# A graph layer on one core: moving the transposes of the attention weights to just in front of each part's sum, two parts ahead, and spreading the logits over four parts

## The chip, the core and the metric

The kernel runs on one core of one Trainium2 chip. The metric is the device time of one execution in microseconds (us). The kernel before takes 1484.36 us, the median of three runs (1482.55 to 1485.34).

The engines named below work side by side, each through its own list of instructions in order: TensorE (PE, matrix products and transposes into PSUM), ScalarE (ACT), VectorE (DVE), GpSimd (POOL), and SyncE, which starts transfers.

## The reference, cut to what matters

```python
def _top_p_attention(X, W1, W2, W3):
    q = X @ W1.T @ W2.T
    k = X @ W3.T
    probs = softmax(q @ k.T, axis=-1)
    # keep, row by row, the largest probabilities until their sum reaches TOP_P = 0.9
    A = probs * mask
    return A / A.sum(-1, keepdims=True)

h = relu(layernorm(x))                    # (3327, 256)
R = (adj + eye) / row sums                # adj is sparse: about 5 entries in a row
Xf = Xa = h; Z = 0
for n in range(2):                        # STEPS = 2
    A = _top_p_attention(Xa, W1, W2, W3)
    Xf = R @ Xf
    Xa = A @ Xa
    Z = Z + Xf @ U1[n].T + Xa @ U2[n].T
return x + layernorm(h + Z) * ln_g + ln_b
```

`A` has 3327 x 3327 entries. The kernel pads the rows to 26 tiles of 128 (`NT = 26`, `NP = 3328`) and never holds `A` as a whole: it goes tile by tile, and for one tile of 128 rows it holds `e`, the 128 x 3328 exponentials of the logits.

## The kernel before: the parts that the change touches

Each of the two steps is one loop over the tiles. One pass of it (an *iteration* `i`) is cut into seven *parts*, `PARTS = 7`. In every part a few pieces of work for different tiles are taken up in the order that a string of letters (`PLAN`) gives; each letter advances one generator to its next `yield`. In iteration `i` of the first step the tile `i` has its threshold found and its weights masked (`d`), the tile `i+1` is measured (`m`), the logits of tile `i+2` are made (`w`), the queries of tile `i+3` are projected (`q`), the tile `i-2` is spread through the sparse matrix (`s`) and finished (`e`), and the sum `A @ Xa` of the tile before is made, four of its 26 column blocks in each part.

```python
AHEAD = (1, 2)
PLAN = (("mdsssa", "mdsssa", "edawwp", "sda", "mpdea", "mdgawwq", "emdgq"),   # first step
        ("cmss", "cnms", "wwnfd", "mdsss", "smwqdfg", "mqdfg", "mwdf"))       # second step
LATE = (1, 4)
    ...
            for k in range(PARTS):
                g = PARTS * (i - 1) + k - LATE[step]
                summing = valid(g // PARTS)
                if summing:
                    sums.turn(g, min(i, NT - 1))
                for c in "bb" + (LAST.get(i, PLAN[1]) if step else PLAN[0])[k]:
                    next(work[c], None)
                if summing:
                    ended = sums.sum(g)
    ...
            for c in "cnwqsepgb" if step else "dmwqsepgb":
                run(work[c])          # what is left of the iteration's work
```

The two functions that make the sum. `turn` transposes 128 x 128 blocks of `e` into a PSUM tile `pt` and lets ACT copy them to `eT` in SBUF; `sum` multiplies with `eT`. The PSUM tile `pt` has two buffers, used in turn by every user of `ps_t`; `eT` has three.

```python
ps_t = ctx.enter_context(tc.tile_pool(name="ps_t", bufs=2, space=PSUM))
ps_l = ctx.enter_context(tc.tile_pool(name="ps_l", bufs=2, space=PSUM))
    ...
def turn(self, g, made):
    while self.turned <= min(g + self.ahead, PARTS * (made + 1) - 1):
        ...
        pt = ps_t.tile([P, 4, P], F32, tag="pt", name="pt")
        for j in range(w):
            PE.transpose(pt[:, j, :], e[:, (j0 + j) * P : (j0 + j + 1) * P], ident)
        eT = tpool.tile([P, 4, P], F32, tag="eT", name="eT", bufs=3)
        S.copy(eT[:, :w, :], pt[:, :w, :])
def sum(self, g):
    ...
    for c in range(4 * k, min(4 * k + 4, NT)):
        PE.matmul(self.pa, eT[:, c - 4 * k, :], self.xa[:, j, :], start=c == 0, stop=c == NT - 1)
    if k < PARTS - 1:
        return None
    S.activation(dst[:n], self.pa[:n], AF.Copy, scale=...)       # xa, the tile's sum
```

The other users of a `pt` buffer, and the work that stands between them, shortened (V is DVE, S is ACT, G is POOL; a `# yield` is where a letter ends):

```python
# w and q: one generator, weights(t): q takes its first two pieces, w the four that follow
PE.matmul(pq[:, 0, :], w2d[qp, :], qry[qp, j, :]); PE.matmul(pm, qry[qp, j, :], qm[...])   # pt
S.copy(qT, pq[:, 0, :]); S.copy(mq, pm)                               # yield
V.scalar_tensor_tensor(mq ...); six small G operations -> ms          # yield
for n in range(4):                                                    # the logits, 832 columns each
    pl = ps_l.tile(...); two PE.matmul(pl[:, a, :416], qT, keys)
    S.activation(e[...], pl, AF.Exp, accum_out=za)                    # yield after each piece
# e: first_end(i - 2)
aT = transposed(r)                  # 2 PE.transpose into pt, S.copy(xT)   yield
PE.matmul(pz, aT, u2) x2            # 512 columns, PSUM tile of its own
S.copy(xw[:, t, :], pz[:, D:]); V.tensor_tensor(sv, pz[:, :D], x0) # yield
PE.matmul(pk ...) x2 (and 2 more in even tiles)    # pt
S.copy(krs) (even tiles); S.copy(keys); S.copy(qry)                   # yield (even tiles)
PE.matmul(pg ...); S.copy(gt)                      # pt, even tiles only
# m: measured_once(tile i + 1)
nine small S operations             # yield
S.activation(ja, e, AF.Relu)        # a pass over 128 x 3328             yield
S.activation(ja, e, AF.Sign)        # a second such pass                 yield
seven small S operations            # yield
five small V operations
# d: settle(tile i), all on V: a pass w over e; ten MAX8; ten MAX8; three rounds; two rounds;
#    the mask e = e * (e >= threshold), a pass over e; two small operations (a yield between each)
# p: packed(i + 1):   PE.matmul(pb) in pt, S.copy                     yield   V operations
# g: gathered(i):     PE.matmul(po) in pt, S.copy(lo)                 yield   V operations, then
#                     ten indirect DMAs on G that fetch the rows of the sparse matrix and of bx
# s: spread(i - 2):   six PE.matmul(pr), a yield after each; then V operations
# a: listed():        one chunk of adj by DMA, V.tensor_reduce        yield
```

All instructions of PE, ACT and DVE keep the order of this text.

Of the kernel before, what the change touches and what calls it, by code (L numbers as in the profile page):

```python
# [22 lines left out]
NT = (N + P - 1) // P  # L23
# [299 lines left out]
SQG, SQK = ((c[0], c[1] / (2 * c[0]), c[2] - c[1] ** 2 / (4 * c[0])) for c in (PG, PK))  # L323
HALF = NT // 2
PARTS = -(-NT // 4)
AHEAD = (1, 2)
COUNTED = [t for t in range(NT - 2) if t % 2 == 0]
EARLY = (11, 18, NT)
FIRST = 8 * P
# [14 lines left out]
def guess_graph_layer(ctx, tc, x, adj, w1t, w2t, w3t, u1t, u2t, ln_g, ln_b, out, flag):  # L344
# [207 lines left out]
    def weights(step, t, live, known=True):  # L552

        r = dict(Z=rec[:, step, 3, t : t + 1])
        qT, r["ms"] = yield from project(step, t, law=known)
        yield
        r["e"] = e = es[(2, 3, 0, 1, 4, 5)[t % 6] if step else t % 4]
        r["za"] = za = small.tile([P, CUT + 1], F32, tag="za", name="za")
        live[step, t] = r
        w = HALF * P  # L560
        wd = w // CUT
        for n in range(CUT):
            c = n * wd
            pl = ps_l.tile([P, 2, 512], F32, tag="pl", name="pl")
            for a in range(2):
                p = slice(a * DA, (a + 1) * DA)
                PE.matmul(pl[:, a, :wd], qT[p, :],  # L567
                          keys[step][p].rearrange("p a b -> p (a b)")[:, c : c + wd],
                          start=True, stop=True)
            if n < CUT - 1:  # L570
                S.activation(e.rearrange("p (a n) -> p a n", a=2)[:, :, c : c + wd], pl[:, :, :wd],  # L571
                             AF.Exp, accum_out=za[:, n : n + 1])
                yield
            else:
                S.activation(e.rearrange("p (a n) -> p a n", a=2)[:, :, c : w - 1], pl[:, :, : wd - 1],
                             AF.Exp, accum_out=za[:, n : n + 1])
                S.activation(e[:, w - 1 : w], pl[:, 0, wd - 1 : wd], AF.Exp, accum_out=za[:, n + 1 :])
# [110 lines left out]
    def measured(step, r):  # L688
        return measured_twice(r) if step else measured_once(r)
# [52 lines left out]
    def prove(step):  # L742
        v8, t, tn, Z = (rec[:, step, k, :] for k in range(4))
        ok = small.tile([P, NT], F32, tag="cum", name="ok", bufs=1)
        o2 = small.tile([P, NT], F32, tag="dr", name="o2", bufs=1)
        V.tensor_tensor(ok, v8, t, ALU.is_lt)
        V.tensor_tensor(o2, tn, t, ALU.is_lt)
        V.tensor_tensor(ok, ok, o2, ALU.mult)
        for a, c, op in ((tn, 0.0, ALU.is_gt), (t, 0.5 * BIG, ALU.is_lt),
                         (Z, 1.0e-30, ALU.is_gt), (Z, BIG, ALU.is_lt)):  # L750
            V.scalar_tensor_tensor(ok, a, c, ok, op, ALU.mult)
        V.tensor_scalar(ok, ok, 0.5, None, ALU.is_lt)
        n = N - (NT - 1) * P
        f = small.tile([P, 1], F32, tag="f", name="f")
        V.tensor_reduce(f, ok[:, : NT - 1], AX.X, ALU.add)
        V.tensor_tensor(fl, fl, f, ALU.add)
        V.tensor_tensor(fl[:n], fl[:n], ok[:n, NT - 1 :], ALU.add)
        if step == 0:
            V.tensor_scalar(ok, lists[:, :, LIST - 1], 0.0, None, ALU.is_gt)
            V.scalar_tensor_tensor(ok, ends, float(P), ok, ALU.is_gt, ALU.add)  # L760
            V.tensor_reduce(f, ok, AX.X, ALU.add)
            V.tensor_tensor(fl, fl, f, ALU.add)
# [121 lines left out]
    def first_end(t):  # L884
        aT = transposed(live.pop(("r", t)))
        yield
        pz = ps_r.tile([P, 2 * D], F32, tag="pr", name="pz")
        for c in range(ND):
            PE.matmul(pz, aT[:, c, :], u2[:, c].rearrange("p n d -> p (n d)"), start=c == 0, stop=c == ND - 1)  # L889
        S.copy(xw[:, t, :], pz[:, D:])  # L890
        sv = row.tile([P, D], F32, tag="sv", name="sv", bufs=2)
        V.tensor_tensor(sv, pz[:, :D], x0[:, t, :], ALU.add)  # L892
        nc.sync.dma_start(sx[t], sv)
        yield
        yield from prep(1, aT, t)
# [32 lines left out]
    def run(work, n=99):  # L928
        for _ in range(n):
            next(work, None)  # L930
# [59 lines left out]
    def spread(step, t):  # L990
        rr = rrs[:, t : t + 1]
        own = row.tile([P, D + 1], F32, tag="own", name="own", bufs=2)
        nc.sync.dma_start(*((own[:, :D], vx[:, t, :]) if step else (own, bx[:, t, :])))
        s1 = row.tile([P, D], F32, tag="s1", name="s1", bufs=4)
        nc.sync.dma_start(s1, (sx if step else ax)[t])
        a, w = acs.pop(t), D + 1 - step
        pr = yield from diffuse(a, xgs.pop(t), own[:, :w], w)
        if step == 0:
            nc.sync.dma_start(cx[t], a.rearrange("p k r -> p (k r)"))
        yield  # L1000
        if step == 0:
            V.reciprocal(rr, pr[:, D : D + 1])
        V.scalar_tensor_tensor(s1, pr[:, :D], rr, s1, ALU.mult, ALU.add)  # L1003
        if step == 0:
            nc.sync.dma_start(vx[:, t, :], s1)
        else:
            live["f", t] = s1

    def refetch(t):
# [7 lines left out]

    PLAN = (("mdsssa", "mdsssa", "edawwp", "sda", "mpdea", "mdgawwq", "emdgq"),  # L1020
            ("cmss", "cnms", "wwnfd", "mdsss", "smwqdfg", "mqdfg", "mwdf"))

    LAST = {NT - 1: ("cfss", "cn", "ndddddd", "sss", "sf", "f", "f"), NT: ("cf", "v", "", "", "f", "f", "fv")}
# [4 lines left out]
    for step in range(2):  # L1028
        sums = Sums(step, live, xw if step else x0, AHEAD[step])

        for i in range(-1, NT + 2):
            if step == 0 and i == NT - 3:
                begun = [weights(1, t, live, False) for t in range(3)]
            if step == 1 and i == -1:
                run(begun[0])
                prove(0)
                for e in es[4:]:
                    G.memset(e[:, N:NP], 0.0)
            work.update(
                n=work["m"],  # L1040
                c=work["d"],
                d=settle(step, i, live[step, i]) if valid(i) else none,
                m=measured(step, live[step, i + 1]) if valid(i + 1) else none,
                s=spread(step, i - 2 + 2 * step) if valid(i - 2 + 2 * step) else none,
                w=later.pop((step, i + 2), none),
                e=first_end(i - 2) if step == 0 and valid(i - 2) else none,
                a=lister if step == 0 and i else none,
                p=packed(i + 1) if step == 0 and i >= 0 and valid(i + 1) else none,
                g=none if not valid(i + 2 * step) else refetch(i + 2) if step else gathered(i),
                b=none, q=none, v=proof() if step and i == NT else none,  # L1050
            )
            if i >= 0 and valid(i + 3):
                later[step, i + 3] = weights(step, i + 3, live)
                work["q"] = itertools.islice(later[step, i + 3], 2)
            if step == 0 and i >= NT - 2 and i < NT + 1:

                work["w"] = itertools.islice(begun[i - NT + 2], CUT - 1)
            if step == 0 and i >= NT - 3 and i < NT:
                work["q"] = itertools.islice(begun[i - NT + 3], 1)
            if i == -1:  # L1060
                work["w"] = itertools.chain(begun[1], begun[2])
            if step == 0 and i < 1:
                work["b"] = itertools.islice(product, EARLY[i + 2] - EARLY[i + 1])
            if step == 1 and i == -1:
                work["g"] = itertools.chain(refetch(0), refetch(1))
            for k in range(PARTS):
                g = PARTS * (i - 1) + k - LATE[step]
                summing = valid(g // PARTS)
                if summing:
                    sums.turn(g, min(i, NT - 1))  # L1070
                for c in "bb" + (LAST.get(i, PLAN[1]) if step else PLAN[0])[k]:
                    next(work[c], None)
                if summing:
                    ended = sums.sum(g)
                    if ended and step == 0:
                        live["r", ended[0]] = ended[1]
                    elif ended:
                        work["f"] = finish(ended[0], live.pop(("f", ended[0])), ended[1])
            for c in "cnwqsepgb" if step else "dmwqsepgb":
                run(work[c])  # L1080
            if step == 0 and i == NT:
                moments(1)
                for t in range(3):
                    live[1, t]["ms"] = returned(project(1, t, queries=False))
# [50 lines left out]
```

## Time and profile before

The profile was taken of one execution of 1556.6 us. A profiled execution is longer than a timed one here, so shares and waits are read from the profile, and the time from the three runs.

| stretch of the profile, us | what runs | PE busy | DVE busy | ACT busy | POOL busy |
|---|---|---|---|---|---|
| 0 to 150 | layer norm, first keys and products | 103.76 | 82.08 | 79.00 | 55.77 |
| 250 to 400 | first step, its middle | 132.00 | 121.79 | 102.18 | 82.21 |
| 800 to 900 | end of the first step | 92.39 | 50.53 | 47.91 | 41.73 |
| 1050 to 1200 | second step, its middle | 136.84 | 134.67 | 132.75 | 130.00 |

The first sum of the first step begins at 152.3 us and its last at 893.7 us (the matmuls `pa<-x,eT`); those of the second step (`pa<-xw,eT`) run from 953.0 us to 1543.5 us. In the middle of the first step an iteration takes 29.0 us: the matmul `pk`, which comes once in an iteration, starts at 466.24 us and, twelve iterations later, at 813.76 us.

A busy share is an average. What the first step waits for is read from the list of waits of each engine and from the timeline of one iteration; the lines of both are shown with the prediction. In a line of the timeline the columns are: start, duration, engine, line of the kernel, operation, output and inputs, count, and in brackets how long the engine had been idle before it and who ended that idle time. A row of several matmuls is merged; since they are pipelined, what a group costs PE is read from the start of one row to the start of the next.

### The profile page before, as it was taken

Reading aid. Unit: us, or ns where it says so; the run is one execution under the profiler, and the core shown is the slowest. Engines: PE = TensorE matmul, PEld = TensorE weight load, DVE = VectorE, ACT = ScalarE, POOL = GpSimd, SP = SyncE. Lnnn points to the kernel's source line nnn. Section 1 sums busy time; section 2 is a strip of 40 time slices with the busy share of each in tenths; the row PEclk is TensorE's granted clock in tenths of the full one; section 3 lists DMA queues with packets and bytes.
Section 4 is the critical chain, followed back from the end, with each engine's and each line's share of the span. In section 5 each row is a group of like instructions: output and inputs, shape, how many; then the busy total and the mean of one; then the engine's idle time right before and its main releaser. Section 6 shows DMA issues by size and latency. Waiting matters only on the chain.

```text
span 1556.6 us, 22648 instructions
## 1 busy us (share of the span) xinstructions
PE 1320.4 (85%) x6495; PEld 988.6 (64%) x6495; DVE 1230.2 (79%) x3837; ACT 1104.6 (71%) x2476; POOL 990.8 (64%) x1489
## 2 busy tenths in 40 slices
PE   5857888888888989979889937989989989998886
PEld 3523666666666667657667725767767667777675
DVE  4457797977988889779787238989888889898894
ACT  5537576676676676767665378988988988988961
POOL 6312555645756646556555156888888888888851
PEclk9978899999999999999999967999999999999998
DMA  7554343533533534434323131221221221222200
GB/s 220 167 163 134 105 139 96 152 105 96 156 109 107 143 105 116 127 106 130 114 65 89 53 88 31 72 79 55 72 75 49 81 67 57 82 65 59 82 18 20
DMA packets 97687, 149.81 MB, mean 96 GB/s; under 512 B 15985, under 2 KB 60528, under 8 KB 97552
## 3 DMA queue, kind: packets, MB, share of 16 engines
q1 hardware_dynamic: 78400, 104.00, 21.7%
q0 software_dynamic: 16640, 42.69, 10.6%
q10 hardware_dynamic: 2512, 1.57, 0.3%
q8 instruction: 54, 0.88, 0.2%
q14 instruction: 81, 0.66, 0.2%
HBM read 120.93 MB, written 27.28 MB: 95 GB/s over the span
## 4 chain that ended last, share of the span: by engine, by line
PE 34%; POOL 23%; ACT 20%; DVE 9%; issue 7%; DMA 4%; another core or an unknown queue 1%; SPq 0%; POOLq 0%; ACTq 0%; DVEq 0%
PE pa L793 15%; ACT ja L600 8%; POOL xg L868 7%; PE pt L779 4%; POOL g L678 4%; PE pr L876 4%; PE pl L567 4%; DMA at<-in_adj 3%; ACT e L571 3%; PE pz L889 2%; ACT eT L781 2%; DVE e L734 1%; PE pk L487 1%; DVE cand L705 1%; POOL rstd L468 1%
## 5 line engine op out<-in xcount | busy, mean ns | idle before, releaser
L781 ACT COPY eT<-pt 128x512 f32<-128x512 f32 (+1 forms) x364 | 201.8, 555 | 226.2 <-PE pt L779 145.9
L793 PE MATMUL pa<-xw,eT 128*128 128x256 f32 x1352 | 331.8, 387 | 29.2 <-ACT xa L800 28.6
L793 PE MATMUL pa<-x,eT 128*128 128x256 f32 x1352 | 348.2, 401 | 5.6 <-ACT eT L781 4.5
L859 POOL DMA_INDIRECT ac<-in_adj,index x130 | 176.7, 1359 | 249.2 <-DVE mq L541 152.3
L600 ACT ACTIVATE ja<-e,g 128x3328 uint8<-128x3328 f32 x106 | 325.8, 3073 | 0.1
L793 PEld LDWEIGHTS pa<-xw,eT 128*128 128x128 f32 x1352 | 250.0, 191 | 91.9 <-ACT xa L800 33.3
L793 PEld LDWEIGHTS pa<-x,eT 128*128 128x128 f32 x1352 | 258.7, 199 | 59.9 <-issue 14.5
L705 DVE MAX8 cand<-w 128x8 f32<-128x168 f32 (+1 forms) x1040 | 251.2, 317 | 0.0
L779 PE MATMUL pt<-ident,e 128*128 128x128 f32 x1144 | 179.9, 278 | 39.5 <-DVE e L734 22.9
L868 POOL DMA_INDIRECT xg<-bx,index x130 | 165.9, 1276 | 47.6 <-issue 33.4
L779 PEld LDWEIGHTS pt<-ident,e 128*128 128x128 f32 x1144 | 143.6, 144 | 79.0 <-issue 32.5
L567 PE MATMUL pl<-k,qT 64*128 64x416 f32 x832 | 186.2, 552 | 4.5 <-ACT qT L531 4.0
L700 DVE SCALAR_TENSOR_TENSOR w<-e,g 128x3328 f32<-128x3328 f32 x44 | 163.9, 3725 | 0.7
L876 PE MATMUL pr<-xg,ac 128*128 128x257 f32 (+1 forms) x520 | 138.6, 390 | 22.8 <-DVE s L1003 20.2
L868 POOL DMA_INDIRECT xg<-vx,index x130 | 128.2, 986 | 44.0 <-issue 35.1
L811 DVE TENSOR_REDUCE fm<-at 128x4 f32<-128x512 f32 (+1 forms) x182 | 115.8, 637 | 49.2 <-DMA at<-in_adj 47.3
L734 DVE SCALAR_TENSOR_TENSOR e<-e,rec 128x3328 f32<-128x3328 f32 x40 | 147.4, 3684 | 0.0
L571 ACT ACTIVATE e<-pl 128x832 f32<-128x832 f32 x132 | 113.4, 867 | 7.5 <-PE pl L567 6.9
L876 PEld LDWEIGHTS pr<-xg,ac 128*128 128x128 f32 x520 | 91.0, 195 | 33.6 <-DVE s L1003 20.5
L567 PEld LDWEIGHTS pl<-k,qT 64*128 64x128 f32 x832 | 71.0, 189 | 51.0 <-issue 41.2
L712 DVE MAX8 bb<-cand 128x8 f32<-128x160 f32 x286 | 92.7, 324 | 6.4
L892 DVE TENSOR_TENSOR sv<-pz,x 128x256 f32<-128x256 f32 x26 | 11.0, 422 | 91.4 <-ACT xw L890 81.2
(226 smaller groups left out, 2213.5 us busy)
## 6 DMA issues: line engine op xcount, KB each, us to landing
at<-in_adj SPq DMA_DIRECT2D x156, 256.0 KB
cx<-ac SPq DMA_DIRECT2D x26, 384.0 KB
ac<-cx SPq DMA_DIRECT2D x26, 384.0 KB
bx<-e SPq DMA_DIRECT2D x26, 128.5 KB
own<-bx SPq DMA_DIRECT2D x26, 128.5 KB
x<-in_x SPq DMA_DIRECT2D x13, 256.0 KB
xr<-in_x SPq DMA_DIRECT2D x26, 128.0 KB
ax<-e SPq DMA_DIRECT2D x26, 128.0 KB
```

What stands on the lines that cost most here:

```text
L567: PE.matmul(pl[:, a, :wd], qT[p, :], keys[step][p].rearrange("p a b -> p (a b)")[:, c : c + wd], start=True, stop=True)
L571: S.activation(e.rearrange("p (a n) -> p a n", a=2)[:, :, c : c + wd], pl[:, :, :wd], AF.Exp, accum_out=za[:, n : n + 1])
L600: S.activation(ja, e, f, bias=guess, scale=sign, accum_out=total)
L700: V.scalar_tensor_tensor(w, e, col(16), e, ALU.is_lt, ALU.mult, accum_out=d2)
L705: V.max(cand[:, 8 * s : 8 * s + 8], w[:, s * SEG : min(NP, (s + 1) * SEG)])
L734: V.scalar_tensor_tensor(e, e, at(1), e, ALU.is_ge, ALU.mult, accum_out=ra)
L779: PE.transpose(pt[:, j, :], e[:, (j0 + j) * P : (j0 + j + 1) * P], ident)
L781: S.copy(eT[:, :w, :], pt[:, :w, :])
L793: PE.matmul(self.pa, eT[:, c - 4 * k, :], self.xa[:, j, :], start=c == 0, stop=c == NT - 1)
L859: G.indirect_dma_start(out=ac[:, k, :], out_offset=None, in_=rows, in_offset=bass.IndirectOffsetOnAxis(ap=index[:, t, k : k + 1], axis=0), ...
L868: G.indirect_dma_start(out=xg[:, k, :w], out_offset=None, in_=rows, in_offset=bass.IndirectOffsetOnAxis(ap=index[:, t, k : k + 1], axis=0))
L876: PE.matmul(pr[:, :w], ac[:, k, :], own if k == KT - 1 else xg[:, k, :w], start=k == 0, stop=k == KT - 1)
```

## The change: what it does and what it is for

Three things change, all in the first step. The transposes are made two parts ahead of the sum, not one. They stand directly in front of the part's sum, behind the other work of the part, and not at the head of the part; so ACT can copy them while PE multiplies. And the four pieces of the logits are made in four different parts (2, 3, 5 and 6) and not in two pairs (parts 2 and 5), so that ACT doesn't get two exponentials at once. With that the plan is arranged anew: the keys of the finished tile (`pk`) move from part 6 to part 5, their product `pg` from the end of the iteration to part 6, and the projection of the queries (`pq`) from part 5 to part 6.

```diff
-AHEAD = (1, 2)
+AHEAD = (2, 2)
@@
-    PLAN = (("mdsssa", "mdsssa", "edawwp", "sda", "mpdea", "mdgawwq", "emdgq"),
+    PLAN = (("mdsssa", "mdsssa", "ewpda", "wsda", "mpdea", "mwedga", "wmdegq"),
             ("cmss", "cnms", "wwnfd", "mdsss", "smwqdfg", "mqdfg", "mwdf"))
@@
             for k in range(PARTS):
                 g = PARTS * (i - 1) + k - LATE[step]
                 summing = valid(g // PARTS)
-                if summing:
+                if summing and step:
                     sums.turn(g, min(i, NT - 1))
                 for c in "bb" + (LAST.get(i, PLAN[1]) if step else PLAN[0])[k]:
                     next(work[c], None)
+                if summing and not step:
+                    sums.turn(g, min(i, NT - 1))
                 if summing:
                     ended = sums.sum(g)
```

## The prediction, made before the changed kernel was run

> **What bounds the kernel now.** I read the busy times by stretch first, then the list of waits of PE, then the timeline of one iteration on PE, ACT and DVE. In the middle of the first step PE is the busiest engine:
>
> ```profile
> 400.00:550.00 150.00, 129.42 (x654) 98.06 (x653) 123.00 (x393) 101.39 (x247) 92.47 (x116) 0.98 0.42 121
> ```
>
> The columns are length, PE, weight loads, DVE, ACT, POOL, clock, DMA share and GB/s. No engine is full: PE is idle for some 20 of 150 us, DVE for 27. So the order of the work and its waits set the pace. The list of PE's waits over 175 to 840 us, which is nearly the whole first step, says which:
>
> ```profile
> PE pq L526 <- ACT eT L781: 37.3, 21, 2.9
> PE pk L487 <- ACT mq L535: 24.2, 15, 2.4
> PE po L844 <- ACT eT L781: 8.2, 6, 1.5
> ...
> PE pk L487 <- ACT qT L531: 3.3, 2, 1.7
> ```
>
> The numbers are us in all, times, longest. None of the four is a wait for data. `pq`, `pk` and `po` each want one of the two `pt` buffers and wait until ACT has copied its last content out. They make 37.3 + 24.2 + 8.2 + 3.3 = 73.0 us in 665 us. An iteration takes (813.76 - 466.24) / 12 = 29.0 us, so these are 23 iterations with 3.2 us each. The first step has 26: some 83 us of the profiled 1556.6 are all that better placing can take from these waits.
>
> The timeline shows how they come about. First PE, then ACT:
>
> ```profile
> 454.70 0.60 PE L779 MATMUL pt<-ident,e 128*128 128x128 f32 x4
> 455.14 1.88 PE L889 MATMUL pz<-u,xT 128*128 128x512 f32 x4
> 456.86 1.89 PE L793 MATMUL pa<-x,eT 128*128 128x256 f32 x8
> 458.59 0.60 PE L779 MATMUL pt<-ident,e 128*128 128x128 f32 x4
> 459.02 0.29 PE L844 MATMUL po<-lists,oh 128*128 128x13 f32 x2
> 459.25 1.67 PE L567 MATMUL pl<-k,qT 64*128 64x416 f32 x8
> 461.65 0.48 PE L526 MATMUL pq<-qry,w2d 64*128 64x128 f32 x2 [0.74 <-ACT eT L781]
> ...
> 462.29 1.99 PE L793 MATMUL pa<-x,eT 128*128 128x256 f32 x8
> 464.12 0.38 PE L779 MATMUL pt<-ident,e 128*128 128x128 f32 x2
> 466.24 0.71 PE L487 MATMUL pk<-xT,wk 128*128 128x128 f32 x4 [1.74 <-ACT mq L535]
> ```
>
> ```profile
> 455.88 3.07 ACT L600 ACTIVATE ja<-e,g 128x3328 uint8<-128x3328 f32 x1
> 458.94 0.36 ACT L890 COPY xw<-pz 128x256 f32<-128x256 f32 x1
> 461.01 0.59 ACT L781 COPY eT<-pt 128x512 f32<-128x512 f32 x1 [1.71 <-PE pl L567]
> 461.50 0.30 ACT L621 ACTIVATE g<-oa,g 128x1 f32<-128x1 f32 x1
> ...
> 465.88 0.31 ACT L535 COPY mq<-pq 128x130 f32<-128x130 f32 x1
> ```
>
> The reader is to see that parts 4 and 5 are heavy for ACT: a pass of 3.07 us, a copy, seven small operations, two exponentials, two copies; PE runs into them through the two buffers. And one thing that the work doesn't explain: the transposes issued by 459.02 were copied only at 461.01, though ACT had ended `xw` by 459.30. In the next iteration it is larger: transposes issued at 481.18, ACT free from 480.38, the copy at 486.30. I call this the late copy: about 2 to 4.5 us, once in an iteration, always near parts 3 to 5. The profile shows no cause. The ten gathers that POOL issues run just then (477.67 to 486.47 us in that iteration), but that is only a coincidence in time so far.
>
> DVE sets a floor. Its pass `w<-e,g` starts at 440.77 and at 466.41 us, 25.64 us apart, with 0.63 us idle in between: 25.0 us of DVE work in an iteration. PE's own work, summed from the spacing of its rows, is: transposes 6 x 0.44 + 0.22 = 2.9, sum 6 x 1.73 + 0.86 = 11.2, sparse matmuls 6 x 0.43 = 2.6, logits 4 x 0.83 = 3.3, `pz` 1.7, and `pq`, `pk`, `pg`, `po`, `pb` and the transposes of `xT` about 2.2 together: 23.9 us.
>
> **What the Trainium skill says.** "TensorE: Matmul & The Clock Gate", Part 2, step-by-step: matmuls stay in program order, only weight loads are pulled ahead. So PE can't go round a matmul that waits for a buffer; the trace agrees, behind the `pq` of 461.65 stood a sum whose `eT` had been there since 455.99. "PSUM — Partial Sum Buffer", Specifications: eight banks of 2 KiB per partition. A `pt` is 4 x 128 x 4 bytes, one bank; with two of two banks for `pl` and one each for the two sums all eight are taken, which is why a third `pt` isn't the simple way out. No run here shows that limit. "Perfetto Trace Analysis", Tensor Engine Instruction: the end of a matmul is estimated, and the semaphore update comes only when PSUM has acknowledged the write. That leaves room for a late copy behind a matmul that looks done; the trace has delays of 0.26 us normally (issued 455.14, copied 455.40) and of 2.0 and 4.7 us in the two cases above.
>
> **The change, part by part.** It removes no work and adds none: 23.9 us on PE, 25.0 on DVE and about 20 on ACT remain. It moves three things.
>
> First, transposes ahead of the sum. In ACT's list nothing changes by this alone: a copy that stood at the head of part k+1 stands now at the end of part k, behind the same work. On PE the transposes pass in front of one sum, so the copy can start 1.73 us earlier, and between a copy's transposes and the next user of a buffer there is always a sum. With nothing else changed this should take nearly all of the waits.
>
> Second, single logits. One exponential (0.85 us) goes from part 2 to 3 and one from 5 to 6; part 3 had ACT idle for 1 to 5 us. Neutral to good.
>
> Third, the new places of `pk` and `pq`, which I work out. Take the end of issue of part 3's transposes as 0. PE: sum 1.73, `pz` 1.72, transposes 0.44 (3.89), sum 1.73, `pl` 0.83 (6.45), `pk` 0.55 (7.00), `po` 0.23 (7.23); the next transposes want the buffer of `pk`. ACT: copy from 0.26 to 0.74, Sign pass 3.06 to 3.80, `xw` 0.26 to 4.06, copy of the part-4 transposes from 4.15 to 4.63, seven small operations 2.36 (461.50 to 463.86) to 6.99, exponential 0.85 to 7.84, keys and queries 2 x 0.27 to 8.38. With 0.15 us from ACT to PE the transposes start at 8.53: **a new wait of 1.3 us**. For the kernel before, the same reckoning from the part-4 transposes: PE is at `pk` after 3.89 + 0.23 + 1.66 + 0.64 + 1.83 + 0.38 = 8.63; ACT ends `mq` at 4.63 + 2.36 + 0.05 + 1.68 + 0.30 = 9.02, so `pk` at 9.17: 0.5 us of wait without a late copy. The other 2.7 of the 3.2 us come from the late copy. So the new plan gives back 0.8 us of what the earlier transposes win.
>
> Now with a late copy of 4.4 us on part 4's transposes. Before: `po` waits until 5.29 (1.4), `pq` until 9.1 (1.9), `pk` until 13.5 (1.5): 4.8. After: its copy ends at 9.03, `po` waits from 7.00 to 9.18 (2.2), keys are copied at 12.8, the transposes wait from 9.41 to 12.95 (3.5): 5.7. If the late copy falls on part 1 instead, the two-part lead takes it: sum 1.73, `xT` 0.3 and `pl` 0.83 stand in front of the next use, and a delay of up to some 2 us costs nothing. Where it will fall I can't tell.
>
> Sum for an iteration: at best 3.2 us of waits fall to the 1.3 of the new wait and 0.2 besides, minus 1.7 us or 44 us over 26 iterations; at worst the late copy stays in part 4, plus 0.9 us or 23 us. I take minus 0.3 us, 8 us in all: **1476 us**.
>
> **Rivals.** (a) The late copy vanishes or is hidden wholly, and the step runs at DVE's floor with a little on top, 26 us in place of 29: 78 us less, some 1406. For it: the two-part lead is meant for just that, and part of the 72 us by which the profiled execution is longer may sit in these waits, so that less is there to gain. Against it: the buffers are still two. (b) The wait moves to the transposes behind `pk`, as worked out, and eats the gain: 1476 to 1508. For it: ACT does the seven small operations and the exponential first, in order. (c) DVE becomes the bound. `q`'s second piece, which needs `mq`, follows its first at once now, with the large pass behind it; the wait for `mq` could be 1 us or more of DVE, which has 4 us free. It makes (a) smaller, not (b) larger.
>
> **Range and chances.** The best case without (a) is 1440, the worst 1508; with some of (a) the low end is 1438. Faster by over 2% needs 1.1 us less in each iteration, which asks that the late copy be mostly hidden: 0.22. Slower by over 2% needs 1.1 us more, past my worst case: 0.1. The rest, 0.68.
>
> **What would show it.** In the waits of PE, `pq` and `pk` should be nearly gone and transposes `pt L779` waiting for ACT's `qry` or `k` copy (line 497 or 496) should stand in their place, 1 to 3.5 us each iteration. ACT's busy time and DVE's in the step should stay; DVE should wait for `mq`. The distance of two `pk` should be 28 to 30 us; 26 would speak for (a). The second step should not move. I am wrong if the transposes don't wait for the keys' copies, or if the late copy goes away with the new order.

## The result, and the profile after

The changed kernel takes **1496.26 us** (median of four runs, 1495.4 to 1496.74). In the same set of runs the kernel before takes 1484.85 us. The ratio is 1.0078 with a 95% interval of 1.006 to 1.0095: a loss of 11.4 us, where a gain of 8 us was forecast.

The runs were made on several chips, on three of the five used for the experiments the kernel before takes about 1570 us and not 1485, and so times are compared only with the kernel before on the same chip, by a ratio that leaves out executions more than 1.5% above the fastest of their kernel.

The busy times by stretch of the changed kernel, with the same columns as in the prediction:

```profile
400.00:550.00 150.00, 142.98 (x733) 105.61 (x732) 139.07 (x451) 114.38 (x280) 89.96 (x126) 1.00 0.48 132
```

Beside the line of before this looks like a gain: PE 142.98 us busy in place of 129.42, DVE 139.07 in place of 123.00. It should have made me suspicious of the line of *before*: that profile is of an execution of 1556.6 us. The waits of PE over 175 to 840 us, again us in all, times, longest:

```profile
PE pt L779 <- ACT qry L497: 23.4, 24, 1.2
...
PE pt L779 <- ACT gt L504: 4.3, 11, 0.4
```

`pq`, `pk` and `po` wait for no buffer any more. In their place the part-5 transposes wait for the buffer of `pk` until ACT has copied the queries out. The timeline of PE and then of ACT at that place:

```profile
437.46 0.97 PE L567 MATMUL pl<-k,qT 64*128 64x416 f32 x4
438.36 0.71 PE L487 MATMUL pk<-xT,wk 128*128 128x128 f32 x4
438.91 0.29 PE L844 MATMUL po<-lists,oh 128*128 128x13 f32 x2
440.41 0.44 PE L779 MATMUL pt<-ident,e 128*128 128x128 f32 x2 [1.21 <-ACT qry L497]
```

```profile
438.68 0.29 ACT L627 ACTIVATE g<-g 128x1 f32<-128x1 f32 x1
438.88 0.84 ACT L571 ACTIVATE e<-pl 128x832 f32<-128x832 f32 x1
...
440.09 0.26 ACT L497 COPY qry<-pk 64x128 f32<-64x128 f32 x1
```

ACT does the last of the seven small operations, the exponential of the part's single piece of logits and then the copies, in order. The wait is 1.21 us in one iteration and 0.74 in the next (even tiles have a longer `pk`).

The mean distance of two sums' ends (the copies `xa<-pa`) in the first step is 25.80 us. In the second step it is 22.68, and 22.7 in the kernel before: the step that the change doesn't touch didn't move. So the question is what the first step of the kernel before really looks like when it takes 1484 us.

### The profile page after: what moved, and what is told of

Same layout as the page of the kernel before. It is cut to its first block, busy times and chain, and to the rows that moved or that the text cites. A ratio compares the mean times of both kernels' runs of the same rounds, so it can differ in the third digit from the quotient of the medians.

```text
span 1493.7 us, 22652 instructions
## 1 busy us (share of the span) xinstructions
PE 1307.2 (88%) x6495; PEld 969.0 (65%) x6495; DVE 1227.8 (82%) x3837; ACT 1108.2 (74%) x2476; POOL 987.6 (66%) x1489
## 3 DMA queue, kind: packets, MB, share of 16 engines
q0 software_dynamic: 16640, 42.69, 11.4%
## 4 chain that ended last, share of the span: by engine, by line
PE 33%; POOL 24%; ACT 24%; DVE 7%; issue 7%; DMA 4%; SPq 0%; ACTq 0%; POOLq 0%; DVEq 0%
PE pa L793 15%; ACT ja L600 10%; POOL xg L868 8%; PE pl L567 5%; PE pr L876 5%; POOL g L678 5%; PE pt L779 5%; ACT e L571 4%; DMA at<-in_adj 3%; ACT eT L781 3%; POOL rstd L468 1%; PE pz L949 1%; POOL xr L906 1%; DVE cand L705 1%; DVE fm L811 1%
## 5 line engine op out<-in xcount | busy, mean ns | idle before, releaser
L793 PE MATMUL pa<-x,eT 128*128 128x256 f32 x1352 | 325.3, 383 | 0.0
L793 PEld LDWEIGHTS pa<-x,eT 128*128 128x128 f32 x1352 | 245.4, 192 | 26.1
L859 POOL DMA_INDIRECT ac<-in_adj,index x130 | 133.1, 1024 | 188.0 <-DVE index L852 139.3
L779 PE MATMUL pt<-ident,e 128*128 128x128 f32 x1144 | 183.5, 281 | 69.9 <-ACT qry L497 23.4
L779 PEld LDWEIGHTS pt<-ident,e 128*128 128x128 f32 x1144 | 138.4, 144 | 129.6 <-issue 57.7
L868 POOL DMA_INDIRECT xg<-bx,index x130 | 181.3, 1394 | 49.7 <-issue 33.3
L567 PE MATMUL pl<-k,qT 64*128 64x416 f32 x832 | 199.7, 565 | 4.3 <-ACT qT L531 3.8
L876 PEld LDWEIGHTS pr<-xg,ac 128*128 128x128 f32 x520 | 94.8, 194 | 36.8 <-DVE s L1003 21.0
L567 PEld LDWEIGHTS pl<-k,qT 64*128 64x128 f32 x832 | 66.8, 188 | 59.7 <-issue 50.6
L575 ACT ACTIVATE e<-pl 128x830 f32<-128x830 f32 x44 | 37.6, 854 | 73.4 <-PE pl L567 73.3
```

The lines of the kernel that those rows point to most:

```text
L567: PE.matmul(pl[:, a, :wd], qT[p, :], keys[step][p].rearrange("p a b -> p (a b)")[:, c : c + wd], start=True, stop=True)
L859: G.indirect_dma_start(out=ac[:, k, :], out_offset=None, in_=rows, in_offset=bass.IndirectOffsetOnAxis(ap=index[:, t, k : k + 1], axis=0), ...
L868: G.indirect_dma_start(out=xg[:, k, :w], out_offset=None, in_=rows, in_offset=bass.IndirectOffsetOnAxis(ap=index[:, t, k : k + 1], axis=0))
L876: PE.matmul(pr[:, :w], ac[:, k, :], own if k == KT - 1 else xg[:, k, :w], start=k == 0, stop=k == KT - 1)
```

## The experiments

### The kernel before once more: which kernel did the first profile show?

The theory at this point: the late copies of the prediction are a property of the execution and not of the kernel, and the first profile was of another kind of execution than the three timed runs. Rival: the late copies are in the kernel before always, the new order took them away, and the loss has another source, large enough to eat 80 us. There is no edit: it is the kernel before, unchanged, on three chips.

> The kernel before, unchanged, for a second profile. Theory A (the late copies belong to that one profiled execution and not to the kernel): the profiled span is near 1483 us, no copy eT starts more than 1 us after its transposes and ACT are both free, and an iteration of the first step takes 25.2 to 25.6 us, not 29. Rival (the late copies belong to the kernel, and the change removed them): the span is near 1556 us again and an iteration takes 28 to 29 us. Timed: ratio 1.000 to the kernel before under both.

> The kernel before, unchanged, for a profile beside runs in which it takes 1485 us. Expected there: no late copy of eT; PE's waits for pq and po gone; only pk waits for the copy mq, about 0.5 us an iteration (the reckoning without late copies); 25.3 us an iteration (25.8 of the changed kernel less 11.4 us over 26). If the waits for pq and po are still there without late copies, my reading of the first profile was right and only their size was off. If the kernel before is at 1570 us, late copies are expected again.

> The kernel before, for its profile. Where it takes 1485 us: no late copies, no waits of PE for pq and po, 0.5 us of wait for pk in an iteration, 25.3 us an iteration. Where it takes 1570: late copies as in the two profiles so far.

Measured: 1571.27 us on the first chip (ratio to the kernel before 0.9995, interval 0.9969 to 1.0021), 1571.11 us on the second (1.001, 0.9987 to 1.0033), 1483.23 us on the third (0.9981, 0.9971 to 0.9992). The last ratio is of a kernel with itself: differences of 0.2% are not read as effects here. The first two profiles came out as the rival has it (spans of 1566.9 and 1568.9 us, with late copies), but there the timed runs take 1570 us as well; the third, of an execution of 1483.1 us, settles it.

I counted in each trace the copies `eT` of the first step that start more than 0.6 us after their transposes have ended and ACT is free. There are 31 in the profile that the prediction read (some 92 us of delay in all), 28 to 30 in each of the other two above 1550 us (some 91 to 93 us), and none in the execution of 1483 us. (The end of a transpose in the trace is modelled, so such a count can be off by two or three.) In every kernel that has any they fall on the fourth to sixth of a tile's seven groups of transposes, which the kernel before makes in parts 3 to 5.

The granted clock differs as well: over 200 to 800 us it was 0.97, 0.95 and 0.95 in the three profiles with late copies and 1.00 in the one without. At 3 to 5% of 600 us that is 18 to 30 us of PE's time at most, by estimate, so the clock alone doesn't make the difference of 85 us. Nor do late copies need the lower clock: `pk` apart, below, has about 10 of them at 1.00. Which of the two brings the other was not separated.

The waits of PE in the execution of 1483 us (200 to 800 us), then those of DVE:

```profile
PE pk L487 <- ACT mq L535: 21.2, 21, 1.1
PE pz L889 <- DVE s L1003: 5.3, 5, 1.7
PE pk L487 <- ACT qT L531: 1.6, 2, 1.1
```

```profile
DVE fm L811 <- DMA at<-in_adj: 11.0, 13, 1.8
```

The waits of `pq` (37.3 us in the first profile) and `po` (8.2) do not exist there. Only the wait in front of `pk` is left, about 1.0 us an iteration. And the chain of work that ended last, cut out of the same profile (start, us, engine, tile, line, count):

```profile
438.14 3.61 DVE e L734 x2
441.78 0.16 DVE ra L735
441.94 0.58 DVE fm L811
...
444.28 3.62 DVE w L700 x2
447.92 0.21 DVE need L701
448.13 0.59 DVE fm L811
448.73 2.28 DVE cand L705 x10
451.00 3.05 DMA at<-in_adj
454.08 0.43 DVE fm L811
...
463.32 3.61 DVE e L734 x2
```

**DVE is the bound.** From one mask pass to the next the chain is DVE and a transfer that DVE waits for: 463.32 - 438.14 = 25.2 us, beside 25.0 us of DVE's own work (in these 25.2 us DVE is busy for 24.15; the rest of its work is short gaps between its instructions). PE's wait of 1.0 us at `pk` lies beside this chain and costs nothing: the kernel `place_only` below hasn't got it, and its iteration is as long. In the first profile the same chain ran mostly over PE (58% of its length between 250 and 700 us, ACT 24%, DVE 9%); in this one DVE has 77% and PE nothing. So the first step of the kernel before, as it was timed, had next to nothing to give to a better order of PE's work.

### The changed kernel once more

> The changed kernel, unchanged, timed again beside the kernel before on one chip. In the last session the kernel before took 1570 us and its profile held 28 late copies of eT (91.6 us in all) in parts 3 to 5 of the first step; the profile of the changed kernel held none. Theory A (late copies come with the chip or the session, and the changed kernel is slower by its buffer wait wherever there are none): if the kernel before is near 1485 here, the changed one is near 1496; if it is near 1570, the changed one has late copies too and lies at 1560 to 1600. Theory B (the new order is free of late copies everywhere): near 1496 in both cases.

> The changed kernel. Where the kernel before takes 1485 us: 1496 again, ratio 1.008. Where it takes 1570: it holds late copies too, and since q_late took 1532 there, 1530 to 1540; then the changed kernel is slower on the one and faster on the other.

Measured: 1496.57 us (1.0091, 1.0074 to 1.0108) and 1496.86 us (1.0067, 1.0044 to 1.0091), without late copies. The second is the median of four, one of which took 1924.12 us; that of the other three is 1496.34 us. The loss is there on both chips where the kernel before takes 1485 us; the changed kernel wasn't run on a chip where that one takes 1570, so what the two expectations say of that stays untested. The chain of the changed kernel, one iteration, from the wait behind `pk` to the next:

```profile
440.09 0.27 ACT qry L497
440.41 0.44 PE pt L779 x2
440.84 1.73 PE pa L793 x8
442.57 0.90 PE pl L567 x4
...
452.52 0.90 PE pl L567 x4
...
455.96 0.92 PE pl L567 x4
456.91 0.59 ACT e L571
...
457.86 0.47 ACT eT L781
458.33 3.04 ACT ja L600 x2
...
465.60 0.27 ACT qry L497
465.91 0.44 PE pt L779 x2
```

The bound has gone over to a **loop of PE and ACT**: the copy of the queries lets PE go on (440.41), PE works through 16.5 us of rows in order up to the logits of part 3 (455.96), ACT takes the exponential of that piece, the copy of the transposes, the Sign pass, the seven small operations, the exponential of part 5 and the copies of keys and queries (456.91 to 465.87, 9.0 us), and PE goes on again. PE has 61 to 62% of the chain between 250 and 700 us, ACT 35%, DVE none. The loop takes 25.5 or 26.4 us by turns, DVE needs 25.0.

### The logits in single pieces alone

The kernel before with nothing but its four logits pieces in four parts (each `w` in a part of its own):

```diff
-    PLAN = (("mdsssa", "mdsssa", "edawwp", "sda", "mpdea", "mdgawwq", "emdgq"),
+    PLAN = (("mdsssa", "mdsssa", "edawp", "swda", "mpdea", "mdgawq", "emwdgq"),
```

> The kernel before with the logits in four single pieces (parts 2, 3, 5 and 6) and nothing else moved. Theory: ACT's two exponentials in part 5 stand in the way of mq, which pk waits for, and so one of them moved to part 6, ahead of nothing that is waited for, should cut the wait of pk from about 0.5 us to 0; but the buffer of pb in part 2 comes one logit piece sooner to PE, and waits for a copy behind the Relu pass, 0.5 to 0.8 us. The reckoning gives plus 0.5 us an iteration, 1490 to 1500 us where the kernel before takes 1485. Rival (single logits are what helps): 1470 to 1480.

Measured: 1500.17 us, 1.0112 (1.0095 to 1.0129): a loss of 15.9 us without any of the rest. The time is at the upper end of the expected range, and the wait of `pb` came; that of `pk` fell from 1.0 to 0.7 us and not to 0:

```profile
PE pk L487 <- ACT mq L535: 14.9, 21, 0.7
PE pb L832 <- ACT eT L781: 10.1, 22, 0.5
```

Its chain, by engine and line:

```profile
by line: ACT ja L600 24.2%; PE pa L793 22.0%; ACT eT L781 8.2%; PE pl L567 7.0%; PE pt L779 5.6%; issue 5.4%; ACT e L571 3.2%; PE pk L487 2.7%; ACT g L622 1.5%; ACT g L592 1.5%; ACT g L623 1.5%; PE pb L832 1.4%; ACT xa L800 1.4%; ACT g L626
```

Again a loop of PE and ACT, now mostly over ACT (54% of the chain between 250 and 700 us, PE 40%), and DVE is off the chain. So single pieces in the order of before cost time by themselves; how much of that is PE's longer rows and how much the other order on ACT this run doesn't tell. What changes on PE is seen from the spacing of the rows (start of a row to the start of the next), averaged over 16 iterations with no late copy:

| us per iteration | before (1483 us) | after | single pieces alone |
|---|---|---|---|
| logits `pl` | 3.10 | 3.55 | 4.03 (some 0.5 of it the wait of the `pb` behind them) |
| `pt`, `pk`, `po`, `pq` together, waits included | 6.20 | 6.21 | 5.74 |
| the rest | 16.24 | 16.22 | 16.38 |
| iteration | 25.54 | 25.98 | 26.15 |

A pair of pieces (eight matmuls) takes 1.51 us or 1.60 us to the start of the next row, a single piece (four matmuls) 0.81 or 0.90 us: two singles take 0.2 us more than a pair. And behind a sum the first logits matmul comes 0.309 us after the last one of the sum, where the next matmul of the sum would come after 0.216. The Trainium skill names a cause, "TensorEngine Tiling (Array Packing)", Tiling Modes, Key Properties: "Mode switching requires drain". The logits' weights have 64 rows, nearly everything around them 128, so a group of them is two switches, and four groups are twice as many as two. The page gives no size; by these rows it is some 0.1 us a switch. That the switch is the cause was not isolated.

### The buffer of the keys taken out of the ring

The changed kernel with `pk` in another PSUM tile in the first step, so that the transposes don't wait for it:

```diff
-        pk = ps_t.tile([P, 4, P], F32, tag="pt", name="pk")
+        if step:
+            pk = ps_r.tile([P, 2 * D], F32, tag="pr", name="pk").rearrange("p (a r) -> p a r", r=P)
+        else:
+            pk = ps_t.tile([P, 4, P], F32, tag="pt", name="pk")
```

(`pr` is the PSUM tile of the sparse sum. `step` is 1 for the keys that the first step's loop makes for the second; the `else` holds for the keys made before the loop.)

> The changed kernel with one edit: in the first step's loop pk takes the PSUM buffer of pr and pz and not one of the two pt buffers, so the transposes of part 5 no longer want the buffer that ACT empties late. Theory A: the wait of the transposes for the copy qry (23.4 us in the changed kernel's profile) is gone, the iteration falls from 25.8 to 24.5 to 25.0 us, and the time is 1465 to 1480 us, under the kernel before. Rival (DVE's new wait for mq, 24.9 us in the profile, is what costs): the wait for qry goes and the time stays at 1490 to 1497 us.

> The changed kernel with pk in the PSUM buffer of pr and pz, where there are no late copies. Theory A (the wait of the transposes behind pk is the loss): 1478 to 1487 us, the kernel before or under it, bound by DVE. Rival (DVE's wait for mq is the loss, it stays as it is here): 1493 to 1497 us. With late copies: near 1497.

> The changed kernel with pk in the PSUM buffer of pr and pz. Twice it took 1492 to 1498 us where the kernel before took 1570; where that takes 1485: theory A (the wait of the transposes behind pk is the loss) 1478 to 1487 us; rival (DVE's wait for mq is the loss) 1493 to 1497 us.

Measured, on the chip that gives 1486 us for the kernel before: 1485.14 us, 0.9991 (0.9983 to 0.9999), which is 11.2 us less than the changed kernel beside it (1496.34 without its execution of 1924 us). PE's waits and the chain there (line numbers are three higher in this kernel):

```profile
PE pk L490 <- DVE sv L895: 8.5, 11, 1.6
PE pt L782 <- ACT gt L507: 4.3, 11, 0.4
```

```profile
by line: DVE e L737 12.8%; DVE fm L814 9.9%; DMA at<-in_adj 9.7%; DVE w L703 8.0%; DVE cand L708 6.7%; DVE cand L717 6.0%; DVE bb L715 5.7%; DMA ac<-in_adj,index 5.6%; PE pa L796 3.2%; issue 3.0%; POOL ac L862 2.9%; DVE s L1006 1.8%; DVE dr
```

The wait for the queries' copy (22.5 us) is gone and DVE is the bound again. So the whole loss goes away with that one wait, though the four single pieces are still there: a PE with 0.45 us more of logits and no wait still fits beside DVE's 25 us. That the buffer closes the loop is thereby shown. That the loop needs the longer way on PE and ACT as well is argued from the sums: no run in which the kernel before takes 1485 us has this buffer wait with pairs of logits.

On the chips that give 1570 us the same kernel takes 1497.68 us (0.9523, 0.945 to 0.9596) and 1492.25 us (0.9533, 0.9487 to 0.9579). Its first steps there have about 10 late copies each, with some 16 and 13 us of delay, and still it is 73 to 77 us faster than the kernel before. The first expectation was too low: an iteration takes 25.5 us there and not 24.5 to 25.0.

### The second piece of the queries later

The rival (c) of the prediction was DVE's wait for `mq`; in the changed kernel DVE does wait for it, over 200 to 800 us:

```profile
DVE mq L541 <- ACT mq L535: 20.8, 21, 1.8
```

Here `q` makes only its first piece in part 6 of the first step, and the second piece moves to part 1 of the next iteration:

```diff
-    PLAN = (("mdsssa", "mdsssa", "ewpda", "wsda", "mpdea", "mwedga", "wmdegq"),
+    PLAN = (("mdsssa", "mdsssaw", "ewpda", "wsda", "mpdea", "mwedga", "wmdegq"),
...
-                work["q"] = itertools.islice(later[step, i + 3], 2)
+                work["q"] = itertools.islice(later[step, i + 3], 2 if step else 1)
```

> The changed kernel with the second piece of q (DVE's small operation on mq and six of GpSimd) put off to part 1 of the next iteration, so that DVE no longer waits for mq at the end of part 6 (20.5 us in the changed kernel's profile); the wait of the transposes for qry stays. Theory A (the buffer wait is the loss): 1494 to 1499 us, as the changed kernel. Rival (DVE's wait for mq is the loss): 1480 to 1487 us.

> The changed kernel with the second piece of q put off to the next iteration. It took 1532 us where the kernel before took 1570. Where that takes 1485: theory A 1494 to 1499 us, as the changed kernel; rival (DVE's wait for mq is the loss) 1480 to 1487 us.

Measured beside 1486.01 us: 1494.06 us, 1.0053 (1.0034 to 1.0072), only some 2 us less than the changed kernel. DVE's wait for `mq` is gone from its list (in part it waits elsewhere now: for `xw`, 22.2 us where it was 12.1); PE's is as it was:

```profile
PE pt L779 <- ACT qry L497: 22.9, 24, 1.2
```

DVE's wait for `mq` was slack, and rival (c) falls. On the chip that gives 1569 us it takes 1532.32 us (0.9776, 0.9731 to 0.9821), with fewer than ten late copies.

### The transposes alone

The changed kernel with the plan of before: the transposes two parts ahead and in front of the sum, `pq` and `pk` and the pairs of logits as they were.

```diff
-    PLAN = (("mdsssa", "mdsssa", "ewpda", "wsda", "mpdea", "mwedga", "wmdegq"),
+    PLAN = (("mdsssa", "mdsssa", "edawwp", "sda", "mpdea", "mdgawwq", "emdgq"),
```

> The transposes directly in front of the sum and two parts ahead, but with the plan of the kernel before (logits in two pairs, pk in part 6, pq in part 5). Theory A (the new plan's buffer wait behind pk makes the changed kernel slower, the new place of the transposes is a gain): the waits of PE for pq, pk and for transposes on the copies of ACT are under 0.3 us an iteration, the iteration takes 24.3 to 25.0 us, and the time is 1462 to 1478 us. Rival (moving the transposes is itself the loss, because they stand between the other work and the sum): 1490 us or more, as the changed kernel.

> Transposes in front of the sum and two parts ahead, plan of the kernel before, where there are no late copies. One part ahead gave 0.9964. Two parts ahead make the first transposes of a tile wait for DVE's mask in part 6, as in turn_pk (26.9 us in its profile), so DVE's 25 us of work are the bound and the time is 1476 to 1486 us. With late copies: 1510 to 1550, as before.

> Only the first part of the change: transposes two parts ahead and directly in front of the sum, the old plan with its pairs of logits. It has been timed only beside executions of the kernel before that took 1570 us. Theory (logits in pairs as before, the two-part lead takes away the waits for the buffer of pt, and DVE's 25.1 us of work an iteration is then the bound): 1476 to 1486 us beside 1485 for the kernel before, logits at 3.1 us an iteration, waits of PE for the buffers of pt under 0.5 us an iteration. Rival (the earlier transposes themselves cost time, by collisions on ACT or POOL): 1490 to 1500.

All three fell on chips that give 1570 us. Measured: 1533.62 us (four runs between 1509 and 1550, no ratio), 1544.6 us (0.9767, 0.9677 to 0.9857) and 1537.09 us (0.9748, 0.9692 to 0.9803). So where late copies are, the first part of the change is a gain: the last of the three has about 20 late copies with some 50 us, where the kernel before has 28 to 31 with some 92. It doesn't end PE's waits for a buffer, as the first expectation had it; in the last of the three the transposes wait for the copy of `po`:

```profile
PE pt L779 <- ACT lo L846: 34.6, 21, 2.7
PE pq L526 <- ACT eT L781: 14.9, 14, 1.8
```

The expectation for 1485 us was not tested by this kernel.

Two others tested it nearly, both with the plan of before. `place_only` keeps the lead of one part; `turn_pk` has the lead of two parts, `AHEAD = (2, 2)`, and `pk` apart as above. The edit of the first, besides the plan:

```diff
-AHEAD = (2, 2)
+AHEAD = (1, 2)
```

> The plan of the kernel before with the transposes in front of the sum but only one part ahead. If the place is the gain and the two parts are not: as fast as or faster than the kernel before by 5 to 25 us (the next sum still comes one part after its transposes). If the second part ahead is needed, because a sum waits for its eT behind a 3.07 us pass of ACT: PE waits for eT at the sum (pa) by 0.5 us or more in an iteration and the time is that of the kernel before or more.

> The plan of the kernel before, the transposes directly in front of the sum and two parts ahead, and pk in the PSUM buffer of pr and pz. Without late copies: no buffer of pt is waited for in an iteration, the iteration takes 24.3 to 25.0 us, 1462 to 1478 us in all, so some 1% under the kernel before. With late copies: some 1490 to 1520, 3 to 5% under it.

Measured beside 1484.26 us: 1478.99 us (0.9964, 0.9948 to 0.9979) for the place alone, 1482.5 us (0.9982, 0.9967 to 0.9997) with the two-part lead and `pk` apart. The waits of PE in the first:

```profile
PE pz L889 <- DVE s L1003: 26.3, 18, 3.0
```

All but 0.2 us of PE's waits for a buffer of `pt` are gone; PE waits for DVE. And yet the iteration is not shorter: the mean distance of two sums' ends in the first step is 25.29 us, where the kernel before has 25.31. The 5.3 us, a ratio only twice as far from 1 as the kernel before from itself, come from the start of the step: in the two profiles the first sum ends at 183.3 us and at 189.9. So the waits for the buffers were worth nothing in the loop. In `turn_pk` the transposes wait for DVE instead (26.9 us) and an iteration takes 25.14 us, where 24.3 to 25.0 were expected. `place_only` is the kernel that beats both.

### The plan alone, and the new places with pairs

The kernel before with nothing but the new plan:

```diff
-    PLAN = (("mdsssa", "mdsssa", "edawwp", "sda", "mpdea", "mdgawwq", "emdgq"),
+    PLAN = (("mdsssa", "mdsssa", "ewpda", "wsda", "mpdea", "mwedga", "wmdegq"),
```

> The new plan alone, with the transposes at the head of the part and one part ahead as before. Theory A: the buffer behind pk is waited for here too, 1 us or more in an iteration, and the time is 1495 to 1510 us, as much as or more than the changed kernel. Rival (the new plan is harmless or good, the new place of the transposes is the loss): 1475 to 1488 us.

Measured on a chip with late copies: 1589.62 us, 1.0125 (1.0097 to 1.0154), with about 26 late copies (some 60 us). PE waits for the queries' copy, as expected, 26.8 us in all and 1.4 us each. The plan costs there too; the expected times, for 1485 us, were not tested.

Last, the changed kernel with its four pieces of logits joined to two pairs, in parts 3 and 6:

```diff
-    PLAN = (("mdsssa", "mdsssa", "ewpda", "wsda", "mpdea", "mwedga", "wmdegq"),
+    PLAN = (("mdsssa", "mdsssa", "epda", "wwsda", "mpdea", "medga", "wwmdegq"),
```

> The changed kernel with the same pieces of logits in two pairs (parts 3 and 6) in place of four single ones (parts 2, 3, 5 and 6); all else as changed. Theory (each group of 64-row logits matmuls costs PE about 0.1 us to enter and leave, so four groups cost 0.45 us an iteration more than two, by the spacing of the rows): the logits fall from 3.55 to about 3.1 us an iteration, an iteration from 25.9 to 25.5 us, and the time to 1485 to 1490 us beside 1485 for the kernel before and 1496 for the changed one, although the transposes still wait for the queries' copy. Rival (the loss is the wait of the transposes for ACT's copies, or DVE's wait for mq, and single logits cost nothing of themselves): 1495 to 1500. If the kernel before takes 1570 us beside it, the theory expects 1500 to 1530 and only the spacing of the rows tells.

Measured: 1602.7 us beside 1567.95, 1.0225 (1.0195 to 1.0256). Both expectations missed. There are few late copies (about 10, with some 14 us); what grew is this:

```profile
PE pt L779 <- ACT qry L497: 50.3, 20, 2.8
PE po L844 <- ACT eT L781: 19.7, 19, 1.9
```

The wait behind `pk` is 2.5 us each where it was 1.0 in the changed kernel, and `po` waits again. In the new order both exponentials of the first pair stand in front of part 3's copy and of the Sign pass on ACT, and in part 5 no logits stand between the sum and `pk` on PE, so PE comes to the buffer sooner and ACT to the queries no sooner. But the run is also disturbed otherwise (the granted clock was 0.93 between 400 and 550 us, the sum's rows take 12.66 us an iteration and not 11.5), so it parts neither of the two. A pair in front of free transposes takes 1.60 us here too, so the row spacing repeats; what the switches alone are worth in the total the run doesn't tell.

## Why the prediction was wrong, point by point

**The step that failed first: "No engine is full ... So the order of the work and its waits set the pace."** That was true of the profiled execution and false of the kernel that was timed. I had the number in hand: the profile's 1556.6 us beside 1484.36. I took it for a cost of profiling ("A profiled execution is longer than a timed one here"), and that is wrong: the profiles taken since agree with timed runs of the same kernel to 1.3% or better (1483.1 beside a median of 1483.23; 1493.7 beside 1496.26). What the timed kernel showed in its place is DVE as the bound, 25.2 us of chain in an iteration of 25.3, with PE's waits slack beside it. I wrote under rival (a) that "part of the 72 us ... may sit in these waits, so that less is there to gain" and then didn't take it out of the sum. In the timed kernel the "83 us" that better placing could take are about 1.0 us an iteration, and these lie beside a chain that is DVE's.

**The late copy** was described rightly (parts 3 to 5, 2 to 4.5 us), and taken for a property of the kernel. It comes with the execution: 28 to 31 in each of the three profiles of the kernel before above 1550 us, none in the one of 1483. (How many there are where they come depends on the order too: about 10 in `pk` apart.) "The other 2.7 of the 3.2 us come from the late copy" was right; but these 2.7 us were not in the time to be beaten. What I credited as a gain was absent there. Where late copies are, the two-part lead took part of them (0.9748 and 0.9767).

**The new wait**: predicted 1.3 us for the transposes behind `pk`, waiting for the keys' and queries' copy; measured 1.21 and 0.74 by turns, at that place and for that copy. This part of the working was right. **The old wait**, "0.5 us of wait without a late copy", measured 1.0: PE is at `pk` 8.2 us after the part-4 transposes and not 8.63 (the logits, for one, take it 1.50 us and not 1.66). So the wait of the new order is no longer than the old one; the rival (b), that it "eats the gain", is right in its place, but there was no gain to eat. That the measured time lies within (b)'s "1476 to 1508" is in part luck: both ends were reckoned from the waits and late copies of the other execution.

**"Logits 4 x 0.83", "Neutral to good"**: this is the term of the sum that has the wrong sign. I took the 0.83 us from pairs (1.66 / 2) and carried them over to singles; a single piece takes 0.90, or 0.81 before `pq`, and the pair 1.51 to 1.60. Four singles are 3.55 us an iteration where two pairs are 3.10. Times 26 iterations the 0.45 us are 11.7 us, and the loss is 11.4. That the two agree is an account of where PE's time lies, not yet a cause: the wait behind `pk` has to be there as well, as `pk` apart shows. Besides, ACT now takes an exponential directly in front of the Sign pass (456.91), which the loop runs through, and I counted that place as free because ACT was idle there.

**DVE's floor** of 25.0 us an iteration was right, and it is the number that the prediction should have been built on: 25.0 x 26 beside 25.3 measured leaves 8 us at the best. The two kernels without buffer waits gained 1.8 and 5.3 us, the latter at the start of the step.

**The checks named**: `pq` and `pk` nearly gone from the waits, yes; the transposes in their place, yes; DVE waits for `mq`, yes, and it didn't matter; the second step unmoved, yes; the distance of two `pk` 28 to 30 us, no. It is 25.8, which I had said would speak for the vanished late copy. It does, but late copies were as absent from the timed kernel before (25.3).

What stays open is what makes the copies late. All 31 late copies of the first profile begin within 2.1 us of the end of one of POOL's gathers; as the gathers follow each other closely there, it is a coincidence in time, as before, and no run took the gathers away. How much of the loss is the drains, and how much the order on ACT, stays open too.

## What to carry to other kernels

Set the span of a profile beside the timed runs before reading it: where the two differ by more than the runs do among themselves, its waits belong to another execution, and what they promise isn't in the time that is compared. Then ask which engine's work fills an iteration by itself; if that is within a few tenths of a microsecond of the iteration, waits of the other engines are slack; a new order has little to gain there, and it can lose, by making a loop of them that is longer than the bound. And each small group of matmuls with another tile shape than its neighbours had a price here, 0.2 us a group, so pieces are not split for free.

## What the runs showed of the hardware that was not expected

The same kernel takes 1483 to 1486 us on two chips and 1568 to 1571 on three others, and the difference lies in the first step (an iteration of 25.3 or of 28.6 us; 22.7 to 22.8 us in the second step on both). Each chip was used at one time only, so whether it is the chip or the time that makes the difference isn't told. Whatever the two-part lead or `pk` apart takes away there is worth more than anything on the other chips: `pk` apart is 0.9523 on one kind and 0.9991 on the other.

Going from 128-row to 64-row weights and back takes PE some 0.2 us by the spacing of rows: 0.90 us for four matmuls of 416 columns, 1.60 for eight, so that two groups of four take 0.20 us more than one of eight.
